# Linear attention on one core: the two PSUM banks of a pair of heads become one tile, and cosine and sine weigh a chunk of both heads in one operation each

## The chip, the cores and the metric

The kernel runs on one core of a Trainium2 chip. The core has five engines that run side by side and meet only at semaphores: TensorE (PE in the profile, with its weight loads as PEld), VectorE (DVE), ScalarE (ACT), GpSimd (POOL) and SyncE (SP, which here only starts transfers). The metric is the device time of one execution in microseconds (us), lower is better.

## The reference

The whole program is four blocks, each an attention-like layer and a feed-forward layer with a layer norm after each. The change lies in the third block's attention, a causal linear attention with 16 heads of 64 features over 4 sequences of 1024 positions:

```python
def cosformer(x, Wq, bq, Wk, bk, Wv, bv, Wo, bo):
    Qp = relu((x @ Wq + bq).reshape(B, T, 16, 64))
    Kp = relu((x @ Wk + bk).reshape(B, T, 16, 64))
    V  = (x @ Wv + bv).reshape(B, T, 16, 64)
    angles = pi / (2 * T) * arange(T)
    cosw, sinw = cos(angles), sin(angles)
    Qc, Qs = Qp * cosw, Qp * sinw
    Kc, Ks = Kp * cosw, Kp * sinw
    # for every position t, over all positions s <= t
    S_cos = cumsum(Kc[s] outer V[s]);  z_cos = cumsum(Kc[s])
    S_sin = cumsum(Ks[s] outer V[s]);  z_sin = cumsum(Ks[s])
    num = Qc @ S_cos + Qs @ S_sin
    den = max(Qc . z_cos + Qs . z_sin, 1e-6)
    return (num / den).reshape(B, T, 1024) @ Wo + bo
```

A position's cosine and sine are the same for all heads and features, so the kernel weighs the values with them before the sum and the result with them after it.

## The kernel before, in words

The stage is `l2_attn`. A *chunk* is 128 positions, a *quarter* two chunks (256 positions), and a *unit* one quarter and one pair of heads (`hp`, 8 pairs). There are 16 quarters, so 128 units. The loop over `t` is a software pipeline written out by hand: in step `t` it issues the projection of unit `t+2`, the key transposes of unit `t+1`, then for unit `t` the matmuls `l2_within` (scores times values inside a chunk) and `l2_before` (query times the state summed over earlier chunks), then scores and state sums of unit `t+1`, then one step of the third block's expert layer where one is ready (`early`), then `l2_out` of unit `t`, and one step of each generator in `side` (the values of the next quarter, the output projection of the last one). TensorE's order is exactly this order (`manual_schedule` for PE alone). The order of the other engines' queues is made by the planner that builds the program, from its own estimate of when each instruction becomes ready.

TensorE leaves the result of a unit in two PSUM banks: `po0` for the first head of the pair, `po1` for the second, each with one buffer. A bank holds, for either chunk, 130 columns: 65 that are to be weighed by the cosine (64 features and the denominator) and 65 by the sine. `l2_out` (L1134 on) takes them out: for each head `i` and each chunk `c`, ScalarE makes `nsin` = sine times its half (L1142, 65 columns a partition), and VectorE makes `num` = cosine times the other half plus `nsin` (L1145). Then VectorE takes the maximum and the reciprocal of the denominators (L1149, L1150) and multiplies (L1151).

The steps that the prediction speaks of, with their lines: `a`, the masked scores, is written by VectorE from the banks `pa0` and `pa1` (L1098), and it comes before `l2_within` of the unit that it belongs to. `state` is written by VectorE from the bank `kp` (L1081, L1083, L1085). The bank `kp` is then filled by the next key transposes (L131), and it is shared with the output of the expert layer; `pa0` and `pa1` are shared with that layer's hidden values (`pa_m` and `kp_mo` in the profile). `cv` is the values: VectorE adds the bias (L1029), ScalarE weighs them by cosine and sine (L1036). ScalarE also makes `r_q` and `r_k` (L1052), `kN` (L1063) and `coT` (L1171). L127 and L131 are helpers that issue matmuls and transposes.

Of the kernel before, what the change touches and what calls it, by code (L numbers as in the profile page):

```python
# [10 lines left out]
F32 = mybir.dt.float32  # L11
I32 = mybir.dt.int32
U32 = mybir.dt.uint32
AF = mybir.ActivationFunctionType
ALU = mybir.AluOpType
# [3 lines left out]
P = 128  # L19
# [14 lines left out]
VW = HD2 + 1  # L34
# [24 lines left out]
class Net:  # L59
# [42 lines left out]
    def load(self, name, shape, pool=None, tag=None, eng=None):  # L102
        pool = pool or self.const
        t = pool.tile(shape, F32, name=f"sb_{name}", tag=tag or f"sb_{name}")
        src = self.io[name]
        (eng or self.nc.sync).dma_start(out=t, in_=src)
        return t
# [811 lines left out]
    def l2_attn(self, load, dispatch, moe):  # L919

        nc, tc = self.nc, self.tc
        NQ = 2
        with ExitStack() as ctx:
            wp = ctx.enter_context(tc.tile_pool(name="cos", bufs=2))
            self.c2["wp"] = wp
            quarters = [  # L930
                dict(b=b, q=q, c0=q * NQ, x=self.xT[b][:, q * NQ * P : (q + 1) * NQ * P])
                for b in range(B)
                for q in range(NC // NQ)
            ]
            units = [dict(Q=Q, hp=hp) for Q in quarters for hp in range(NP2)]
            self.psq = {}
            for t, n in dict(pj=2, po0=1, po1=1, pr=1).items():
                self.psq[t] = ctx.enter_context(
                    tc.tile_pool(name=f"ps_{t}", bufs=n, space=bass.MemoryType.PSUM)
                )  # L940

            two = ctx.enter_context(
                tc.tile_pool(name="ps_two", bufs=1, space=bass.MemoryType.PSUM)
            )
            for t in (("pa0", "m0"), ("pa1", "m1"), ("kp", "mo")):
                v = two.tile([P, 512], F32, name="_".join(t))
                self.psq.update({t[0]: (v, 0), t[1]: (v, 3 * P if t[0] == "kp" else 2 * P)})
            self.mtags = dict(t="pj", h=("m0", "m1"), o="mo")
            self.l2_tiles(quarters[0], None)
            for f in self.l2_values(quarters[0]):  # L950
                pass
            n = len(units)
            side = []

            def early(moe):

                if "done" not in self.m2["st"][1]:
                    for k in range(1):
                        next(moe)


            ctx.enter_context(tc.manual_schedule(engines={mybir.EngineType.PE}))
            for t in range(-2, n + 4):
                if t == 0:
                    load()
                if 0 <= t + 2 < n:
                    u = units[t + 2]
                    self.l2_project(u)
                if 0 <= t + 1 < n:
                    u = units[t + 1]  # L970
                    if u["hp"] == 0:
                        i = (t + 1) // NP2
                        if i + 1 < len(quarters):
                            nxt = quarters[i + 1]
                            self.l2_tiles(nxt, quarters[i])
                            side.append(self.l2_values(nxt))
                    self.l2_keys(u)
                if 0 <= t < n:
                    self.l2_within(units[t])
                    self.l2_before(units[t])  # L980
                if 0 <= t + 1 < n:
                    self.l2_scores(units[t + 1])
                    self.l2_sums(units[t + 1])
                if "put" in self.m2["st"][0] if t > 0 else False:
                    early(moe)
                if 0 <= t < n:
                    self.l2_out(units[t])
                    if t % NP2 == NP2 - 1:
                        Q = units[t]["Q"]
                        side.append(self.l2_project_out(Q))  # L990
                        if Q["c0"] + NQ == NC:
                            side[-1] = chain(side[-1], dispatch(Q["b"]))
                for g in side[:]:
                    if next(g, self) is self:
                        side.remove(g)
            for g in side:
                for f in g:
                    pass
# [104 lines left out]

    def l2_within(self, u):
        Q, hp = u["Q"], u["hp"]
        u["po"] = [self.psb(f"po{i}", [P, 2, 2 * VW], f"po{i}") for i in range(2)]
        for i in range(2):
            for c in range(2):
                self.nc.tensor.matmul(  # L1109
                    out=u["po"][i][:, c, :],  # L1110
                    lhsT=u["a"][:, i, c, :],
                    rhs=Q["v"][c][:, 2 * hp + i, :, :].rearrange("p a d -> p (a d)"),
                    start=c == 0,
                    stop=False,
                    skip_group_check=True,
                )

    def l2_before(self, u):

        Q, hp = u["Q"], u["hp"]  # L1120
        for c in range(1 if Q["q"] == 0 else 0, 2):
            s = slice(c * P, (c + 1) * P)
            for i in range(2):
                h = self.HALF[i]
                self.nc.tensor.matmul(
                    out=u["po"][i][:, c, :],
                    lhsT=u["q"][h, s],
                    rhs=Q["st"][h, hp, c, :],
                    start=False,
                    stop=True,  # L1130
                    skip_group_check=True,
                )

    def l2_out(self, u):  # L1134
        nc, Q, hp, wp = self.nc, u["Q"], u["hp"], self.c2["wp"]
        trig, po = self.c2["trig"], u["po"]
        num = wp.tile([P, 2, 2, VW], F32, name="num")
        for i in range(2):
            for c in range(2):
                k = Q["c0"] + c  # L1140
                t = wp.tile([P, VW], F32, name="nsin", bufs=4)
                nc.scalar.activation(  # L1142
                    t, po[i][:, c, VW : 2 * VW], AF.Copy, scale=trig[:, k, 1:2]
                )
                nc.vector.scalar_tensor_tensor(  # L1145
                    num[:, c, i, :], po[i][:, c, 0:VW], trig[:, k, 0:1], t, ALU.mult, ALU.add
                )
        dn = wp.tile([P, 2, 2, 1], F32, name="dn")
        nc.vector.tensor_scalar_max(dn, num[:, :, :, HD2 : HD2 + 1], 1e-6)  # L1149
        nc.vector.reciprocal(dn, dn)  # L1150
        nc.vector.tensor_mul(  # L1151
            Q["o"][:, :, hp * P : (hp + 1) * P].rearrange("p c (i d) -> p c i d", d=HD2),
            num[:, :, :, 0:HD2],
            dn.to_broadcast([P, 2, 2, HD2]),
        )
# [981 lines left out]
```

## Time and profile before

| what | value |
|---|---|
| time before, median of 4 runs | 2424.82 us (2420.73 to 2429.36) |
| the profiled execution's own time | 2429.53 us |
| its span, first to last instruction | 2427.7 us |
| mean granted TensorE clock in it | 0.910 |
| PE busy over the span | 2084.1 us (86%), PEld 1458.9 us (60%) |
| DVE busy | 1439.8 us (59%) |
| ACT busy | 1334.4 us (55%) |
| POOL busy | 860.5 us (35%) |
| the attention stage, first to last `po` matmul | 646.3 to 1387.2 us |

A row of the profile names a line of the kernel, an engine, an operation and the tiles (output `<-` inputs, buffer numbers left out), then a count, the busy time and the mean duration of one in ns, and the idle time of that engine just before, with what ended it. The numbers that belong to this stage are read from windows of the trace, since shares of the whole span mix stages with different limits. Two `po` rows, `po0` and `po1`, appear as one name.

### The profile page before, as it was taken

Reading aid. Unit: us, or ns where it says so; the run is one execution under the profiler, and the core shown is the slowest. Engines: PE = TensorE matmul, PEld = TensorE weight load, DVE = VectorE, ACT = ScalarE, POOL = GpSimd, SP = SyncE. Lnnn points to the kernel's source line nnn. Section 1 sums busy time; section 2 is a strip of 40 time slices with the busy share of each in tenths; the row PEclk is TensorE's granted clock in tenths of the full one; section 3 lists DMA queues with packets and bytes.
Section 4 is the critical chain, followed back from the end, with each engine's and each line's share of the span. In section 5 each row is a group of like instructions: output and inputs, shape, how many; then the busy total and the mean of one; then the engine's idle time right before and its main releaser. Section 6 shows DMA issues by size and latency. Waiting matters only on the chain. (4 is left out here: it accounts for less than half of the span.)

```text
span 2427.7 us, 35395 instructions
## 1 busy us (share of the span) xinstructions
PE 2084.1 (86%) x12170; PEld 1458.9 (60%) x12170; DVE 1439.8 (59%) x4207; ACT 1334.4 (55%) x2934; POOL 860.5 (35%) x557
## 2 busy tenths in 40 slices
PE   6677879979899999999989965777888989798988
PEld 3455654544577777787768754553455646465666
DVE  7447733433466666755555656676778777676421
ACT  6643433332456566656655555657667776666443
POOL 5001220000000011001021137868888989678400
PEclk9657969979999999999989977987999999898999
DMA  3000110023000010021223156663567766575411
GB/s 101 0 18 22 31 30 9 9 70 86 1 2 1 1 34 21 17 75 42 69 65 88 46 150 189 207 183 91 150 181 186 204 167 183 151 202 153 116 58 48
DMA packets 138516, 209.87 MB, mean 86 GB/s; under 512 B 18597, under 2 KB 75936, under 8 KB 138080
## 3 DMA queue, kind: packets, MB, share of 16 engines
q1 hardware_dynamic: 126048, 172.82, 23.9%
q0 software_dynamic: 12288, 34.79, 6.8%
q8 instruction: 96, 1.57, 0.3%
q14 instruction: 84, 0.69, 0.1%
HBM read 159.24 MB, written 23.16 MB: 75 GB/s over the span
## 5 line engine op out<-in xcount | busy, mean ns | idle before, releaser
L1798 POOL TENSOR_TENSOR hc<-db,cn 128x1024 f32<-128x1024 f32 x128 | 320.4, 2530 | 79.4 <-PE pys L127 30.8
L1782 POOL TENSOR_TENSOR db<-ud,bn 128x1024 f32<-128x1024 f32 x128 | 329.2, 2606 | 44.6 <-DVE pmv L159 16.6
L127 PEld LDWEIGHTS py<-wh,hh 128*128 128x128 f32 x2048 | 249.7, 193 | 80.9 <-issue 41.9
L127 PE MATMUL ph<-xT,wh 128*128 128x512 f32 x512 | 264.4, 637 | 21.0 <-DVE h_acc L1926 6.6
L127 PE MATMUL py<-wh,hh 128*128 128x128 f32 x2048 | 256.5, 278 | 16.3 <-ACT hh L1910 16.0
L1145 DVE SCALAR_TENSOR_TENSOR num<-po,sb_c_trig,nsin 128x65 f32<-128x65 f32 x512 | 132.7, 279 | 231.6 <-ACT nsin L1142 217.7
L1910 ACT ACTIVATE hh<-ph,sb_cols 128x512 f32<-128x512 f32 x256 | 171.2, 681 | 142.8 <-PE ph L127 116.3
L1142 ACT ACTIVATE nsin<-po,sb_c_trig 128x65 f32<-128x65 f32 x512 | 147.9, 315 | 177.3 <-DVE num L1145 103.7
L1786 ACT ACTIVATE da<-dl,aneg 128x512 f32<-128x512 f32 x256 | 175.4, 689 | 72.7 <-DVE db L1787 70.9
L1019 POOL MEMSET cv<- 128x16 f32 x32 | 4.0, 127 | 499.5 <-ACT cv L1036 355.5
L127 PE MATMUL pys<-hc,sb_c_ident 128*128 128x512 f32 x320 | 167.6, 653 | 15.2 <-DMA hc<-hc 15.2
L1926 DVE SCALAR_TENSOR_TENSOR h_acc<-py,gt,h_acc 128x128 f32<-128x128 f32 x256 | 71.9, 343 | 154.4 <-PE py L127 154.4
L127 PEld LDWEIGHTS ph<-xT,wh 128*128 128x128 f32 x512 | 93.3, 202 | 114.2 <-issue 61.0
L1787 DVE TENSOR_TENSOR_SCAN db<-da,carry,db 128x512 f32<-128x512 f32 x128 | 156.8, 1267 | 5.9 <-ACT da L1786 4.3
L1787 DVE TENSOR_TENSOR_SCAN db<-da,db 128x512 f32<-128x512 f32 x128 | 149.8, 1207 | 10.6 <-ACT da L1786 7.9
L127 PE MATMUL pqk<-xT,wE 128*128 128x256 f32 x512 | 136.2, 389 | 7.4 <-DVE cv L1029 6.0
L1359 POOL DMA_INDIRECT xrows<-xN,di x64 | 61.9, 968 | 220.6 <-ACT kN L1063 215.7
L1109 PE MATMUL po<-cv,a 128*128 128x130 f32 x1024 | 136.2, 276 | 0.9 <-DVE num L1145 0.9
L1109 PEld LDWEIGHTS po<-cv,a 128*128 128x128 f32 x1024 | 124.7, 191 | 2.6 <-issue 1.0
L1036 ACT ACTIVATE cv<-cv,sb_c_trig 128x520 f32<-128x520 f32 x128 | 86.4, 724 | 52.1 <-DVE cv L1029 46.7
L127 PEld LDWEIGHTS pys<-hc,sb_c_ident 128*128 128x128 f32 x320 | 63.5, 211 | 84.4 <-issue 62.8
L127 PEld LDWEIGHTS pqk<-xT,wE 128*128 128x128 f32 x512 | 87.6, 190 | 25.1 <-DVE cv L1029 10.1
(430 smaller groups left out, 4445.8 us busy)
## 6 DMA issues: line engine op xcount, KB each, us to landing
wx<-in_wF SPq DMA_DIRECT2D x92, 384.0 KB
wh<-in_wH SPq DMA_DIRECT2D x64, 512.0 KB
bn<-rows SPq DMA_DIRECT2D x128, 256.0 KB
cn<-rows SPq DMA_DIRECT2D x128, 256.0 KB
hc<-hc POOLq DMA_DIRECT2D x48, 512.0 KB
xrows<-zero SPq DMA_DIRECT2D x4, 1472.0 KB
xg<-xrows SPq DMA_DIRECT2D x20, 256.0 KB
yrows<-ys SPq DMA_DIRECT2D x20, 256.0 KB
```

Of the source, the lines that this page charges most:

```text
L127: return self.nc.tensor.matmul(out=out, lhsT=lhsT, rhs=rhs, start=start, stop=stop)
L1036: nc.scalar.activation(Q["v"][c][:, hs, i, :], v1[:, hs, :], AF.Copy, scale=c2["trig"][:, k, i : i + 1],)
L1109: self.nc.tensor.matmul(out=u["po"][i][:, c, :], lhsT=u["a"][:, i, c, :], rhs=Q["v"][c][:, 2 * hp + i, :, :].rearrange("p a d -> p (a d)") ...
L1142: nc.scalar.activation(t, po[i][:, c, VW : 2 * VW], AF.Copy, scale=trig[:, k, 1:2])
L1145: nc.vector.scalar_tensor_tensor(num[:, c, i, :], po[i][:, c, 0:VW], trig[:, k, 0:1], t, ALU.mult, ALU.add)
L1359: i = nc.gpsimd.indirect_dma_start(out=rows[:, :], out_offset=bass.IndirectOffsetOnAxis(ap=st["dest"][k][:, c : c + 1], axis=0), in_=self. ...
L1782: nc.gpsimd.tensor_mul(db, ud, bc[0])
L1786: nc.scalar.activation(da, dl[:, ec, :], AF.Exp, scale=aneg[:, j : j + 1])
L1787: nc.vector.tensor_tensor_scan(db[:, ec, :], da, db[:, ec, :], carry[:, ec, n : n + 1] if h else 0.0, ALU.mult, ALU.add,)
L1798: nc.gpsimd.tensor_mul(hc, db, bc[1])
L1910: nc.scalar.activation(ht, ph, AF.Relu, bias=self.col("h_b1", i=e * NK + k))
L1926: nc.vector.scalar_tensor_tensor(acc[:, c, :], py[:, c, :], gt[:, c, e : e + 1], acc[:, c, :], ALU.mult, ALU.add,)
```

## The change

The two banks of a unit are one tile of two banks, in one pool `po` with one buffer, so PSUM use stays at eight banks. The matmuls that fill it are the same, in the same order. `l2_out` no longer loops over heads: for each chunk, one ScalarE operation weighs the sine half of both heads (2 x 65 columns, from both banks) and one VectorE operation weighs the cosine half of both and adds. A unit has two of each where it had four of each, each of twice the columns. The temporary `nsin` is twice as wide, with two buffers in place of four.

```diff
-            for t, n in dict(pj=2, po0=1, po1=1, pr=1).items():
+            for t, n in dict(pj=2, po=1, pr=1).items():
...
     def l2_within(self, u):
         Q, hp = u["Q"], u["hp"]
-        u["po"] = [self.psb(f"po{i}", [P, 2, 2 * VW], f"po{i}") for i in range(2)]
+
+        po = self.psq["po"].tile([P, 2, 512], F32, name="po")
+        u["po"] = po[:, :, 0 : 4 * VW].rearrange("p i (c d) -> p i c d", c=2)
         for i in range(2):
             for c in range(2):
                 self.nc.tensor.matmul(
-                    out=u["po"][i][:, c, :],
+                    out=u["po"][:, i, c, :],
...
-                    out=u["po"][i][:, c, :],
+                    out=u["po"][:, i, c, :],
                     lhsT=u["q"][h, s],
                     rhs=Q["st"][h, hp, c, :],
...
         num = wp.tile([P, 2, 2, VW], F32, name="num")
-        for i in range(2):
-            for c in range(2):
-                k = Q["c0"] + c
-                t = wp.tile([P, VW], F32, name="nsin", bufs=4)
-                nc.scalar.activation(
-                    t, po[i][:, c, VW : 2 * VW], AF.Copy, scale=trig[:, k, 1:2]
-                )
-                nc.vector.scalar_tensor_tensor(
-                    num[:, c, i, :], po[i][:, c, 0:VW], trig[:, k, 0:1], t, ALU.mult, ALU.add
-                )
+        for c in range(2):
+            k = Q["c0"] + c
+            t = wp.tile([P, 2, VW], F32, name="nsin")
+            nc.scalar.activation(t, po[:, :, c, VW : 2 * VW], AF.Copy, scale=trig[:, k, 1:2])
+            nc.vector.scalar_tensor_tensor(
+                num[:, c], po[:, :, c, 0:VW], trig[:, k, 0:1], t, ALU.mult, ALU.add
+            )
```

## The prediction

> **What bounds the kernel now.** I read the page first, then busy times of the attention stage alone, then what TensorE waited for in it, then the timeline of single units.
>
> ```profile
> L1145 DVE SCALAR_TENSOR_TENSOR num<-po,sb_c_trig,nsin 128x65 f32<-128x65 f32 x512 | 132.7, 279 | 231.6 <-ACT nsin L1142 217.7
> L1926 DVE SCALAR_TENSOR_TENSOR h_acc<-py,gt,h_acc 128x128 f32<-128x128 f32 x256 | 71.9, 343 | 154.4 <-PE py L127 154.4
> L1142 ACT ACTIVATE nsin<-po,sb_c_trig 128x65 f32<-128x65 f32 x512 | 147.9, 315 | 177.3 <-DVE num L1145 103.7
> L1036 ACT ACTIVATE cv<-cv,sb_c_trig 128x520 f32<-128x520 f32 x128 | 86.4, 724 | 52.1 <-DVE cv L1029 46.7
> ```
>
> The page shows the two changed operations as long waits on each other: 217.7 us of VectorE idle before num, 103.7 us of ScalarE idle before nsin. The question is whether TensorE feels it. The busy times from 646 to 1390 us answer that (columns: length, then PE, PEld, DVE, ACT, POOL busy, clock, DMA):
>
> ```profile
> 646.00:1390.00 744.00, 700.01 (x5992) 573.87 (x5990) 461.41 (x1877) 445.20 (x1255) 73.73 (x104) 0.99 0.13 36
> ```
>
> TensorE is busy 700.0 of 744 us; VectorE 62%, ScalarE 60%. Shorter work on those two can return at most TensorE's 44.0 us of idle time, 1.8% of the kernel. TensorE's waits in this window say who ends it:
>
> ```profile
> PE pa_m L127 <- DVE a L1098: 8.1, 11, 1.5
> PE kp_mo L131 <- DVE state L1085: 7.5, 18, 1.9
> PE pqk L127 <- DVE cv L1029: 6.0, 12, 0.6
> PE kp_mo L127 <- ACT kN L1063: 5.9, 8, 2.4
> PE kp_mo L127 <- DVE state L1085: 5.8, 4, 2.3
> ...
> PE po L1109 <- DVE num L1145: 0.9, 1, 0.9
> ```
>
> Only 0.9 us stand against num itself. The others are VectorE and ScalarE work that shares a queue with num and nsin. The timeline of one unit without side work (start, length) shows how:
>
> ```profile
> 713.71 0.32 ACT L1142 ACTIVATE nsin<-po,sb_c_trig 128x65 f32<-128x65 f32 x1 [1.19 <-PE po L1125]
> ...
> 714.06 0.28 DVE L1145 SCALAR_TENSOR_TENSOR num<-po,sb_c_trig,nsin 128x65 f32<-128x65 f32 x1 [1.41 <-ACT nsin L1142]
> 714.26 0.75 DVE L1098 TENSOR_TENSOR a<-pa_m,sb_c_tri 128x256 f32<-128x256 f32 x2
> 714.38 0.52 ACT L1142 ACTIVATE nsin<-po,sb_c_trig 128x65 f32<-128x65 f32 x2 [0.35 <-DVE num L1145]
> ...
> 714.92 0.47 DVE L1145 SCALAR_TENSOR_TENSOR num<-po,sb_c_trig,nsin 128x65 f32<-128x65 f32 x2
> 715.30 0.28 DVE L1083 TENSOR_TENSOR state<-kp_mo,state 128x130 f32<-128x130 f32 x1
> 715.42 0.32 ACT L1142 ACTIVATE nsin<-po,sb_c_trig 128x65 f32<-128x65 f32 x1 [0.52 <-DVE num L1145]
> 715.62 0.29 DVE L1085 TENSOR_TENSOR state<-kp_mo,state 128x130 f32<-128x130 f32 x1
> ```
>
> Here the two engines take turns: the second nsin waits 0.35 us until the first num is done, though both read other columns of the same bank. VectorE's order is num, a, num, num, state, state, num; the last num ends at 716.11, 2.76 us after the unit's last `po` matmul started (713.35). Read the same way for all 128 units, the commonest length of this chain is 2.76 us, and about ten units have 4.1 to 7.8 us. In units with side work the next `po` matmul starts 1.1 us or more after the chain's end; in the others it starts 0.14 us after it or up to 0.37 us before (the first bank is already free).
>
> **The change, part by part.**
>
> *ScalarE.* Out: 512 x 315 ns = 161.3 us. In: 256 operations of 130 columns. Between 65 columns (315) and 520 (724, same kind of scale operand) the slope is 0.90 ns a column, so 315 + 65 x 0.90 = 373 ns; 95.5 us. It saves 66 us of an engine that is 60% busy: nothing by itself, since TensorE covers it; it counts where a TensorE wait ends on ScalarE (kN 5.9, ys 2.0, coT 1.4 us). Bounds of the duration: 315 (columns free) and 2 x 315 = 630 (two banks read one after the other); I take 373, nearest to the L1036 row.
>
> The Trainium skill puts it a little higher: "ScalarE: Activation LUTs", section "What ACT_TABLE_LOAD costs", gives 280 ns + 0.833 ns a column with one pointer operand, 388 ns here. For 65 columns it would be 334, where this trace has 315. By the page a unit saves 560 ns of ScalarE, by the rows 514; both are hidden, so the forecast is the same.
>
> *VectorE.* Out: 512 x 279 = 142.8 us. In: 256 x 345 ns (L1926, the same operation with a column operand and a PSUM input, has 343 at 128 columns) = 88.3 us. 54 us less on an engine that is 62% busy, hidden in the same way. Bounds 279 and 558.
>
> *The chain.* In the unit above, with VectorE's order kept: nsin 713.71 to 714.08, num 714.13 to 714.48, a from 714.40 to 715.15, the second nsin 714.52 to 714.89, the second num 715.07 to 715.42, then the states at 715.33 and 715.65. The chain ends 0.69 us sooner. The last state ends at 715.94, where it ended at 715.91: the first num is 0.07 later by nsin's and num's added columns, the dropped num gives that back. So the transposes into kp that wait for it, the 0.25 us of this unit, stay.
>
> *The buffer.* One tile is free for the next unit only when its last num is done, and the first nsin needs the last matmul of both heads (at most one `po` matmul, 0.13 us between starts, later). In 24 units `po` is now filled before the last num ends, by 6.0 us together (1.35 in one, 0.07 to 0.37 in the rest). With the chain 0.69 shorter only one of them still waits, by 0.66 us at most.
>
> The Trainium skill speaks against this part: "Perfetto Trace Analysis", "Optimizing Tensor Performance", "Matmuls" wants independent matmul groups to rotate through different PSUM banks, so that the evacuation of one overlaps the next group's matmuls, and the change gives up just that. By the rule alone the 6.0 us above would be lost; by the rows the shorter chain more than covers them.
>
> *The sum, on TensorE's waits, VectorE's order kept.*
> - state (7.5 + 5.8 + 1.4 us): the short ones stay; in the few long ones (up to 2.3 us) VectorE had a backlog, and 0.4 us a unit leaves it: 6 x 0.4 = 2.4, taken as -2.5. Bounds 0 and -14.7.
> - cv (6.0 us, 12 waits): in units with values the last num stands right before it and is gone: 0.2 us each, -2.4. Bounds 0 and -6.0.
> - ScalarE's kN, ys, coT (9.3 us, 12 waits): one operation of 0.32 less ahead of the late ones, two longer by 0.06: some 0.15 each, -1.5 rounded down. Bounds 0 and -9.3.
> - num: the 0.9 us wait goes, and in some 20 units without side work `po` starts right behind num instead of 0.06 sooner: -0.9 - 1.2 = -2.1. Bounds +0.7 and -2.1.
> - a (8.1 us on 11 waits; 17.6 us on 32 weight loads): a stands behind the first num, which is 0.07 to 0.2 later: 11 to 32 x 0.12 = +1.3 to +3.8; I take +2. Bounds +6 and, if a comes ahead of num, -8.1.
>
> Sum: -2.5 - 2.4 - 1.5 - 2.1 + 2 = -6.5 us. The bounds add up to +6.7 and -40. From the profiled 2429.53 us (span 2427.7 and 1.8 around it) that is 2423.0; that execution was 4.7 us above the median of the four, so against the median 2424.82 it is 2418.3. Later stages start on this stage's data, so I carry the gain to the end one to one. 0.3% is 7.3 us, about what a measurement of this kernel tells from no change.
>
> **Rivals.**
>
> *The planner moves a and state ahead of num.* The first nsin is longer, so num becomes ready later, while a is ready at 714.1 in the unit above. In that order a runs 714.1 to 714.85, num at 714.77, state by 715.7, 0.25 us sooner. Then the waits on a (8.1) and more than half of those on state (14.7) go: another -8 - 9 us, 2401. For it: VectorE stands idle for 1.41 us before the first num, next to ready work. Against it: in the order of before the num went first, by a margin that I can't see.
>
> *It does nothing.* TensorE is 94% busy, 1.0 of the clock; if the waits on state, a and cv stay, the time is 2424.8 within 3 us. For it: nearly all that is saved lies on idle engines.
>
> *Slower: the first nsin loses its place in ScalarE's queue.* It needs all eight matmuls of two banks, so the planner may see it ready later and put a coT copy (0.57 us) or other work ahead. VectorE's first num then holds a and state up by as much. The unit at 1202.99 shows the price: nsin came 1.39 us after the last matmul started, the chain took 5.67 us and TensorE waited 1.53 us for a. The place is the part with expert work (from about 1020 us on, near 60 units), where pa and kp are shared and a is awaited in 32 units. At 0.57 us in 30 of them it costs 17 us; with the gains on cv, ScalarE and num (-6) the time is 2436. It decides from 0.25 us a unit. Against it: in most units nsin starts 0.36 us after the last `po` matmul with ScalarE idle before.
>
> **How the numbers follow.** Order kept, small gain: 0.42, around 2418 (2412 to 2424), half beyond 0.3%. a and state ahead: 0.18, 2395 to 2412. Nothing: 0.15, 2422 to 2428. Slower: 0.25, 2430 to 2445. Faster is 0.21 + 0.18 = 0.39, same 0.21 + 0.15 = 0.36, slower 0.25. The range leaves a tenth out on each side: 2400 to 2438; the bounds of the sum alone reach from 2385 to 2432.
>
> **What would show it.** nsin and num x256 each, near 373 and 345 ns; VectorE and ScalarE 54 and 66 us less busy in the stage; the commonest chain near 2.07 us; TensorE busy still near 700 us in a stage of some 738. Right at state: the short waits of 0.25 us are still there. Wrong: a wait of TensorE on num above a few us (the buffer), waits on a above 20 us (the slower rival), or waits on a and state both under 5 us (the first rival); or a stage that is as predicted while the time after it has moved, since the planner orders that part too.

## The result, and the profile after

| | median | runs | range |
|---|---|---|---|
| before | 2423.29 us | 70 | 2413.65 to 2434.22 |
| changed | 2420.03 us | 44 | 2411.25 to 2435.75 |

The ratio is 0.9987, with a 95% interval of 0.9977 to 0.9996: the change saves 1 to 6 us of 2423, less than the 0.3% that the prediction takes for what one measurement can tell from no change. The profiled execution took 2419.40 us, with a span of 2417.6 us.

On the page of the changed kernel (columns: line, engine, operation, tiles, shapes, count, then busy us and mean ns of one, then idle time before and what ended it) the two new operations are these:

```profile
L1143 ACT ACTIVATE nsin<-po,sb_c_trig 128x130 f32<-128x130 f32 x256 | 94.6, 369 | 134.5 <-PE po L1127 75.2
...
L1144 DVE SCALAR_TENSOR_TENSOR num<-po,sb_c_trig,nsin 128x130 f32<-128x130 f32 x256 | 89.2, 349 | 275.1 <-ACT nsin L1143 257.2
```

The 130 columns out of two banks cost 369 and 349 ns, where 65 columns cost 315 and 279. The prediction's estimates, without a surcharge for the second bank, were 373 and 345, so none is to be seen. VectorE's busy time in `num` falls from 132.7 to 89.2 us and ScalarE's in `nsin` from 147.9 to 94.6.

The timeline of the changed kernel shows the same chain as the prediction's unit, in another unit without side work (start, length, then engine, line, operation; in brackets the idle time of the engine and what ended it):

```profile
705.65 0.37 ACT L1143 ACTIVATE nsin<-po,sb_c_trig 128x130 f32<-128x130 f32 x1 [1.22 <-PE po L1127]
...
706.05 0.35 DVE L1144 SCALAR_TENSOR_TENSOR num<-po,sb_c_trig,nsin 128x130 f32<-128x130 f32 x1 [2.00 <-ACT nsin L1143]
706.32 0.75 DVE L1098 TENSOR_TENSOR a<-pa_m,sb_c_tri 128x256 f32<-128x256 f32 x2
706.44 0.37 ACT L1143 ACTIVATE nsin<-po,sb_c_trig 128x130 f32<-128x130 f32 x1 [0.42 <-DVE num L1144]
...
706.98 0.35 DVE L1144 SCALAR_TENSOR_TENSOR num<-po,sb_c_trig,nsin 128x130 f32<-128x130 f32 x1
707.24 0.29 DVE L1083 TENSOR_TENSOR state<-kp_mo,state 128x130 f32<-128x130 f32 x1
...
707.56 0.29 DVE L1085 TENSOR_TENSOR state<-kp_mo,state 128x130 f32<-128x130 f32 x1
...
707.91 0.44 PE L131 MATMUL kp_mo<-sb_c_ident,r_k 128*128 128x128 f32 x2 [0.27 <-DVE state L1085]
```

VectorE's order is the one before with two `num` fewer. The chain from the last `po` matmul to the last `num` is now 2.06 us in most units (2.76 before). But TensorE waits for the second `state`, not for `num`, and that wait is still there: 0.27 us where it was 0.25.

What the stage gained is read best from units 0 to 99, ahead of the third block's first gather. These are windows of TensorE, the kernel before and then the changed one (window, its length, then busy us of PE, PEld, DVE, ACT and POOL, the granted clock, the DMA share and GB/s):

```profile
646.26:1202.99 556.73, 532.12 (x4576) 433.30 (x4574) 348.97 (x1397) 335.83 (x937) 41.31 (x68) 1.00 0.09 26
```

```profile
639.60:1190.58 550.98, 531.17 (x4575) 433.48 (x4574) 310.11 (x1197) 298.82 (x737) 41.18 (x68) 1.00 0.09 27
```

VectorE and ScalarE lose 39 and 37 us of busy time; the units get 5.75 us shorter. This gain is not spread over the units. In the common unit `state` comes as late after the last `po` matmul as before (unit 5: 1.98 and 2.29 us, 1.96 and 2.28 before), and the unit is up to 0.02 us longer. Eight units give 5.69 of the 5.75 us: 39 (1.64), 4 (1.07), 71 (0.94), 84 (0.66), 73 (0.58), and 8, 53 and 74 (0.27 each); in the pair of second profiles, b0_before and e8_after below, the same eight give 5.67. In unit 4 the `num` wait of 0.9 us is gone: before, the last `nsin` of unit 3 stood behind `r_q` and `r_k` on ScalarE (665.85 us), and with the shorter chain it stands ahead of them. In unit 39 TensorE's waits were these before, and then with the change:

```profile
PE kp_mo L127 <- ACT kN L1063: 0.8, 1, 0.8
PE pqk L127 <- ACT coT L1171: 0.7, 1, 0.7
PE kp_mo L131 <- DVE state L1085: 0.6, 1, 0.6
```

```profile
PE pqk L127 <- ACT coT L1170: 0.7, 1, 0.7
```

There ScalarE also works for the router: it loads a function table (ACT_TABLE_LOAD, 1.28 us) and makes `rt_l`. Before, both stand behind the unit's `r_k` and hold up `kN`; with the change they are done ahead of `r_q`. e1_swap below, which merges nothing, has them ahead too, and its unit 39 takes 6.09 us (5.87 in the change, 7.51 before); e3_a_first, with the merged operations, has them behind, and its unit takes 7.51 again. So these 1.6 us come from the place of one table load, which the planner chose, and not from the merging as such.

The whole stage gets only 3.2 us shorter (739.5 to 736.3), since units 100 to 106 lose 2.5 (68.5 to 71.1). There the timeline of the changed kernel has, at the first gather:

```profile
1224.74 0.40 ACT L1521 ACTIVATE yg<-yg,wt 128x128 f32<-128x128 f32 x1 [3.44 <-DMA yg<-yrows,di]
1225.05 0.35 ACT L1143 ACTIVATE nsin<-po,sb_c_trig 128x130 f32<-128x130 f32 x1
1225.43 0.35 DVE L1144 SCALAR_TENSOR_TENSOR num<-po,sb_c_trig,nsin 128x130 f32<-128x130 f32 x1 [6.55 <-ACT nsin L1143]
1225.70 0.75 DVE L1098 TENSOR_TENSOR a<-pa_m,sb_c_tri 128x256 f32<-128x256 f32 x2
...
1226.17 2.08 PE L127 MATMUL pa_m<-xgT,wx 128*128 128x128 f32 x8 [2.72 <-DVE a L1098]
```

`yg` is the scaling of rows that a transfer gathers. In the kernel before, the unit's first `nsin` stood ahead of it on ScalarE; now `yg` stands first, waits 3.44 us for the transfer, and `nsin`, `num`, `a` and TensorE wait behind it. The planner turned the two round. The kernel before was held up in the same unit too, one step later: its `yg` stood ahead of the second `nsin`, and TensorE waited for `state` instead of `a`:

```profile
1237.15 0.40 ACT L1522 ACTIVATE yg<-yg,wt 128x128 f32<-128x128 f32 x1 [2.67 <-DMA yg<-yrows,di]
...
1238.86 1.13 PE L127 MATMUL kp_mo<-wx,mh 128*128 128x128 f32 x4 [2.27 <-DVE state L1085]
```

So the new order moves this wait more than it adds to it. In units 100 to 106 TensorE's idle time rises by 0.7 us (12.6 to 13.3); the other 1.8 of the 2.5 us are the same matmuls at a lower granted clock (56.0 us busy at 0.90, 57.8 at 0.88).

TensorE's waits over the whole stage of the changed kernel (us in total, times, longest) are these:

```profile
PE pa_m L127 <- DVE a L1098: 14.9, 33, 2.7
PE kp_mo L131 <- DVE state L1085: 6.9, 17, 1.9
PE pqk L127 <- DVE cv L1029: 6.4, 13, 0.6
PE kp_mo L127 <- ACT kN L1063: 3.9, 5, 2.4
PE kp_mo L127 <- DVE state L1085: 2.6, 2, 1.4
```

Nothing waits for `num` any more. Waits on `a` went from 8.1 us on 11 waits to 14.9 on 33; those on `state` from 14.7 to 10.5. These lists hold waits above 0.15 us. With the shorter ones the waits on `a` are 9.6 us on 32 before and 14.9 on 34 after, so they are nearly all the same waits, each some 0.15 us longer (in units 0 to 99 the same 17), and those on `state` (L1083 and L1085) go from 17.7 on 54 to 10.6 on 21. The two belong together: in a unit such as 77 TensorE waited 0.07 us for `a` and then 0.08 for `state`, and now waits 0.21 for `a` and no longer for `state`.

### The profile page after: what moved, and what is told of

It reads as the page before. It is cut to its first block, busy times and chain, and to the rows that moved or that the text cites. A ratio compares the mean times of both kernels' runs of the same rounds, so it can differ in the third digit from the quotient of the medians.

```text
span 2417.6 us, 34784 instructions
## 1 busy us (share of the span) xinstructions
PE 2076.3 (86%) x12170; PEld 1456.5 (60%) x12170; DVE 1401.8 (58%) x3951; ACT 1287.8 (53%) x2678; POOL 860.3 (36%) x557
## 5 line engine op out<-in xcount | busy, mean ns | idle before, releaser
L1797 POOL TENSOR_TENSOR hc<-db,cn 128x1024 f32<-128x1024 f32 x128 | 326.9, 2582 | 89.7 <-PE pys L127 33.1
L1144 DVE SCALAR_TENSOR_TENSOR num<-po,sb_c_trig,nsin 128x130 f32<-128x130 f32 x256 | 89.2, 349 | 275.1 <-ACT nsin L1143 257.2
L1143 ACT ACTIVATE nsin<-po,sb_c_trig 128x130 f32<-128x130 f32 x256 | 94.6, 369 | 134.5 <-PE po L1127 75.2
L127 PEld LDWEIGHTS ph<-xT,wh 128*128 128x128 f32 x512 | 93.2, 201 | 116.2 <-issue 60.6
L127 PEld LDWEIGHTS pqk<-xT,wE 128*128 128x128 f32 x512 | 87.6, 190 | 25.5 <-DVE cv L1029 10.5
```

The source lines that it names most:

```text
L127: return self.nc.tensor.matmul(out=out, lhsT=lhsT, rhs=rhs, start=start, stop=stop)
L1143: nc.scalar.activation(t, po[:, :, c, VW : 2 * VW], AF.Copy, scale=trig[:, k, 1:2])
L1144: nc.vector.scalar_tensor_tensor(num[:, c], po[:, :, c, 0:VW], trig[:, k, 0:1], t, ALU.mult, ALU.add)
L1797: nc.gpsimd.tensor_mul(hc, db, bc[1])
```

## The experiments

The kernels ran on three chips, each beside runs of the kernel before on the same chip, and each ratio is to those. The kernel before took 2393.46 us beside e0 to e3, 2395.33 beside b0, e5, e7 and e8, and 2424.94 beside e4, e9, e10 and b1. "Stage" is first `po` matmul to the last unit's first one, "behind" the time from there to the end, both from one profile.

| run | ratio to before, 95% | stage | units 100 to 106 | behind |
|---|---|---|---|---|
| before, the first profile | 1 | 739.5 | 68.5 | 1041.9 |
| b0_before | 1.0009 (0.9991 to 1.0027) | 739.7 | 68.8 | 1028.5 |
| b1_before | one run | 740.6 | 68.6 | 1038.6 |
| changed, the first profile | 0.9987 (0.9977 to 0.9996) | 736.3 | 71.1 | 1041.7 |
| e0_again | 0.9958 (0.9939 to 0.9977) | 732.9 | 67.8 | 1018.0 |
| e8_after | 0.9944 (0.9923 to 0.9966) | 733.2 | 68.1 | 1021.3 |
| e1_swap | 0.9983 (0.9967 to 0.9999) | 747.3 | 65.3 | 1013.9 |
| e2_tile_only | 1.0215 (1.0190 to 1.0240) | 793.4 | 64.7 | 1013.2 |
| e3_a_first | 0.9943 (0.9922 to 0.9965) | 725.8 | 63.8 | 1028.4 |
| e5_yg_behind | 0.9887 (0.9865 to 0.9910) | 722.2 | 54.0 | 1023.1 |
| e7_both | 0.9936 (0.9918 to 0.9955) | 717.4 | 52.8 | 1033.5 |
| e9_busy | 0.9987 (0.9971 to 1.0003) | 735.8 | 71.1 | 1036.4 |
| e4_dve_only | 1.0048 (1.0029 to 1.0067) | 743.0 | 70.1 | 1048.9 |
| e10_before_yg | 1.0036 (1.0008 to 1.0065) | 746.4 | 60.6 | 1047.0 |

### The change again, and the kernel before again

No edit: the two kernels as they are, two runs of each.

> The changed kernel as it stands, in a second profile. If the 3.5 us that the unit at the expert layer's first gather (15.90 us long against 12.42 before) lost come from the order of ScalarE's queue (the scaling of the gathered rows stands ahead of the first nsin), that unit is 15 to 16 us again and TensorE's waits on a are again near 15 us. If they were chance of one execution, the unit is 12 to 13 us and those waits are near 10 us. Ratio to before 0.998 to 0.9995 under both.

> The change once more, beside the two runs below. Stage 732 to 737 us, TensorE's waits on a 14 to 15 us, ratio to before 0.995 to 0.9995.

> The kernel before as it stands, for a second profile of it beside the runs below: which of its stages differ from execution to execution. If the attention stage is set by fixed orders, it is again 737 to 741 us long (first to last unit's first po matmul) and only its units around the gathers move by 1 to 3 us, while the stages before and after it follow the granted clock. If the stage moves as the others do, a difference of 3 us in it between two single profiles says nothing.

> The kernel before once more, to see which stretches come back the same. The attention stage: 739.5 to 739.9 us again. The stretch behind it, up to the end, was 1041.9 and 1028.5 us in the two executions of this kernel, 1041.7, 1018.0 and 1021.3 in the three of the changed one. If it belongs to the order of the program and the chip, it is 1027 to 1030 here beside about 1020 for the change; if it is chance of the execution, it is anywhere between 1015 and 1042.

Measured: on the two chips where the kernel before takes 2393 to 2395 us the change is worth 0.4 to 0.6%, where it was 0.13% in the first comparison. Units 0 to 99 agree to 0.02 us: 556.61 to 550.84 here, -5.77, against -5.75 in the first pair of profiles. What differs lies elsewhere. Both ratios are below what was expected (0.998 and 0.995 at the least). Units 100 to 106 give 0.7 here (b0_before and e8_after, one chip) and lost 2.5 there, though `yg` stood ahead of the change's first `nsin` both times: the unit at the first gather takes 15.90 us in the first profile of the change, 14.26 in e0_again and 12.71 in e8_after, and 12.42, 14.68 and 12.57 in the three of the kernel before, while the waits on `a` are 14.4 to 15.0 us each time the change ran. So the order costs waits on `a`, but the loss of 2.5 us is not shown to come from it. Behind the stage the change gained 7.2 us on the chip that ran both, 10.5 across the two faster chips, and nothing in the first pair. Two executions of one kernel there differ by 3.3 us (1018.0 and 1021.3; 1041.9 and 1038.6), and by chip the same kernel before takes 1028.5 or about 1040. The change also reorders that stretch, though it edits nothing in it: by operation and tiles, VectorE's 1334 operations behind the stage stand in one order in b0_before and b1_before, while the longest order that b0_before and e8_after have in common holds 1113. So chance, the chip and the planner's order may all have a part there, and the profiles don't part them.

### One part of the change alone

e2_tile_only has the two banks as one tile and keeps the four operations of 65 columns on each engine:

```diff
-        u["po"] = [self.psb(f"po{i}", [P, 2, 2 * VW], f"po{i}") for i in range(2)]
+        po = self.psq["po"].tile([P, 2, 512], F32, name="po")
+        u["po"] = po[:, :, 0 : 4 * VW].rearrange("p i (c d) -> p i c d", c=2)
```

> One tile of two banks as in the change, but the four nsin and four num of before, in their order. If one tile for two banks has a price of its own (both engines take turns over the whole tile, and TensorE can fill none of it before the last num is done), the chain grows from 2.76 to about 3.4 us, some 50 units have less spare time than that, TensorE waits on num for 15 to 30 us and the kernel is 10 to 30 us slower than before. If banks and tiles do not matter here, it is within 3 us of before.

It is 2.15% slower, and the stage is 54 us longer. The largest row of TensorE's waits in its stage, and two rows of a unit without side work:

```profile
PE po L1111 <- DVE num L1147: 50.1, 55, 2.4
```

```profile
752.14 0.28 DVE L1147 SCALAR_TENSOR_TENSOR num<-po,sb_c_trig,nsin 128x65 f32<-128x65 f32 x1 [0.38 <-ACT nsin L1144]
...
752.57 1.13 PE L1111 MATMUL po<-cv,a 128*128 128x130 f32 x8 [0.42 <-DVE num L1147]
```

With one tile the two engines never read it side by side: in the timeline each `nsin` starts after the last `num` has ended and the other way round, four times over, so the chain is 3.40 us. And the next unit's matmuls wait for the whole tile. The rule that the prediction weighed against the change ("Perfetto Trace Analysis", "Optimizing Tensor Performance", "Matmuls" in the Trainium skill: let independent matmul groups rotate through PSUM banks, so that emptying one overlaps filling the next) agrees with this run: the two banks are still filled in turn, but come free only together, and TensorE waits 50.1 us for them, where it waited 0.9 before. The merged operations, which shorten the chain by 1.34 us, are what makes one tile bearable: with them TensorE waits for `num` nowhere.

e1_swap has the kernel before with its two loops exchanged (chunk outside, head inside), so two tiles and four operations each, in the order of the change:

```diff
-        for i in range(2):
-            for c in range(2):
+        for c in range(2):
+            for i in range(2):
```

> The kernel before with its two loops exchanged: chunk outside, head inside. Still two tiles, four nsin and four num a unit, so no operation is saved; but consecutive operations now go to different banks, so the two engines need not take turns. If the shorter chain is what pays, the commonest chain (last po matmul to the last num's end) falls from 2.76 to about 2.4 us and the time by 1 to 4 us, near that of the change. If the saved operations pay (54 us of VectorE, 66 us of ScalarE), the time stays within 1 us of before.

The chain falls to 2.25 us by this alone, since successive operations read different banks. But VectorE's order becomes num, num, a, a, and the stage is 7.7 us longer than before: waits on `a` are 16.7 us on 33, and on `state` 19.5. A shorter chain at the price of a later `a` and `state` (each some 0.2 us) loses in the stage. (The kernel as a whole is 0.17% faster: the stretch behind the stage was 14.6 us shorter than in b0_before, which ran on the other of the two faster chips. Why is not settled.)

### Is it the freed engine time, or the place in the queue?

e9_busy is meant to give engine time back without touching the chain: behind the second `nsin`, and behind `co`, the unit's last VectorE operation, two operations each that write tiles nobody reads.

```diff
+        for c in range(2):
+            busy = wp.tile([P, 2], F32, name="busyA")
+            nc.scalar.activation(busy, t[:, c, 0:2], AF.Copy, scale=trig[:, k, 1:2])
+            busy = wp.tile([P, 2], F32, name="busyV")
+            with self.tc.issue_after(last):
+                nc.vector.scalar_tensor_tensor(
+                    busy, num[:, c, 0, 0:2], trig[:, k, 0:1], num[:, c, 1, 0:2], ALU.mult, ALU.add
+                )
```

> The change, with two operations more on ScalarE (2 columns, behind the second nsin) and two more on VectorE (2 columns, behind co, the last operation of the pair) for every pair of heads; they write tiles that nobody reads. By the slope of the rows one of 2 columns takes about 316 - 63 x 0.90 = 260 ns on ScalarE and about 215 ns on VectorE, so the stage gets back some 66 us of ScalarE and 55 us of VectorE, about what the change took out, but none of it lies in the chain from the last po matmul to the last num. If the chain and the place of num ahead of state is what the change is worth, the chain stays at 2.06 us and the stage at 733 to 735 us, with the time within 0.2% of the change's (ratio to the kernel before about 0.995). If the worth is in the freed engines (the backlog that my terms for state, cv and ScalarE are built on), the stage goes back to 737 to 740 us, and the waits on state, cv and kN rise again to those of before (14.7, 6.0 and 5.9 us).

They took 294 ns on ScalarE and 215 on VectorE. Units 0 to 99 (columns as above):

```profile
641.96:1192.96 551.00, 531.97 (x4575) 434.69 (x4574) 335.15 (x1397) 345.95 (x937) 41.36 (x68) 1.00 0.09 27
```

ScalarE is busier than in the kernel before (346 against 336 us), and VectorE has 25 of its 39 us back. The units take 551.00 us, as in the change (550.98), and over the whole stage it took 735.8 us, between the two expected ranges, because units 100 to 106 took 71.1, as in the first profile of the change. The ratio is 0.9987, that of the change.

But the equal length is a sum of parts that cancel, so the run does not show that the freed time is worth nothing. The first `nsin` starts 0.32 us after the last `po` matmul, where it starts 0.38 after it in the change; why is not known. The chain is 2.00 us instead of 2.06, and 50 units are some 0.06 us shorter each, 3.0 us together. Against that, units 71, 84, 79 and 40 are 1.8 us longer; 71 and 84 lose 0.78 and 0.52 of the 0.94 and 0.66 that the change had gained there. Unit 53 is 1.5 us longer at a granted clock of 0.71, unit 0 is 0.3 shorter. So of the gain of 5.75 us some 1.3 to 1.8 can be freed engine time, in units where work of other layers queues on ScalarE and VectorE; in the other units giving it back costs nothing. The rest goes with the shorter chain and with orders such as that of the table load in unit 39, which e9_busy keeps.

### Where `a` stands

e3_a_first is the change with both `num` issued behind `a` on VectorE:

```diff
+            with self.tc.issue_after(self.masked):
                 nc.vector.scalar_tensor_tensor(
                     num[:, c], po[:, :, c, 0:VW], trig[:, k, 0:1], t, ALU.mult, ALU.add
                 )
```

> The change, with VectorE's queue ordered so that the masked scores a stand ahead of both num (the planner puts the first num ahead of a). TensorE's waits on a, 14.9 us in the change, should fall below 5 us, the states come 0.1 to 0.2 us sooner, the last num ends 0.2 to 0.3 us later. If those waits are what is left to gain, the time is 5 to 12 us below the change (2408 to 2415 where the change has 2420). If they are only moved on to state, kN or po, it is within 3 us of the change.

TensorE's waits in its stage:

```profile
PE pa_m L127 <- DVE a L1098: 5.2, 5, 1.3
...
PE po L1111 <- DVE num L1145: 3.8, 11, 0.5
PE kp_mo L131 <- DVE state L1085: 2.8, 4, 1.8
```

The waits on `a` fall from 14.9 to 5.2 us. The stage is 7.1 us shorter than in e0_again: 3.3 in units 72 to 99, beside the expert layer, and 4.0 in units 100 to 106. In units 0 to 71 1.4 us are lost: TensorE now waits 1.9 us for `num` there, and unit 39 is 1.6 us longer, with the table load behind `r_k` again. The time, though, equals that of the change (2382.11 and 2382.56 us): the stretch behind the stage was 10 us longer. This is the order of the prediction's first rival, forced: VectorE goes a, a, num, state, state, num, and `state` comes 0.3 us sooner. The 17 us that the rival put on top came as 7 in the stage and as nothing in the time.

Across units 72 to 99 the medians tell what the order does. Counted from the last `po` matmul's start, the first bank of `a` is done after 1.33 us before, 1.46 in the change, 1.35 in e4_dve_only below and 1.17 here, and in these units TensorE waits for `a` for 3.2, 4.7, 3.6 and 1.3 us, short waits included.

### The gather

e5_yg_behind is the change with `yg` ordered behind the unit's last `nsin` on ScalarE, and the output operations of the unit ahead of the expert layer's step in code order:

```diff
+                if 0 <= t < n:
+                    self.l2_out(units[t])
                 if "put" in self.m2["st"][0] if t > 0 else False:
                     early(moe)
...
+                    with self.tc.issue_after(self.nsin):
                         nc.scalar.activation(
```

> The change, with l2_out issued ahead of the expert layer's step (TensorE's order stays as it is) and the scaling of the gathered rows (yg) ordered behind the unit's nsin on ScalarE. If the place of yg ahead of the first nsin is what the change lost, the unit at the first gather falls from 14.3 to 15.9 us to 11 to 12.5, the seven units around it by 3 to 5 us together, and the time by 2 to 4 us against the change. If ScalarE's queue would be waiting there anyway, the seven units stay within 1 us.

Units 104 to 106, of e8_after and then of e5_yg_behind, from the same chip (columns as above):

```profile
1209.17:1247.72 38.55, 30.15 (x202) 24.73 (x201) 20.51 (x93) 22.98 (x59) 15.70 (x18) 0.82 0.25 68
```

```profile
1210.13:1234.59 24.46, 23.76 (x202) 20.10 (x201) 16.17 (x79) 13.47 (x35) 7.80 (x10) 1.00 0.30 85
```

The same 202 matmuls take 38.55 and 24.46 us. 7.7 us of the 14.1 are idle time of TensorE; the other 6.4 are slower matmuls, 30.15 us busy at a granted clock of 0.82 against 23.76 at 1.00. The expectation was 3 to 5 us for the seven units; 14.1 came. This is the fastest kernel of all: 2370.95 us, 1.13% below the kernel before and about 0.5% below the change on that chip. It was measured on that chip alone, and the two parts of the edit, the code order and the place of `yg`, were not tried apart.

e10_before_yg makes the same edit in the kernel before.

> The kernel before (two tiles, four operations each), with the gathered rows' scaling yg ordered behind the unit's last nsin on ScalarE and with the pair's output operations issued ahead of the expert layer's in code order: the edit that took 14 us from units 100 to 106 of the changed kernel (68 to 54 us). If that gain has nothing to do with the change, the same units fall from 68.6 to 54 to 57 us here, the stage from 739.6 to 725 to 729, and the ratio to the kernel before is 0.990 to 0.995. If the gain needs the change's order (yg stands ahead of the first nsin only there), the units stay at 66 to 69 us and the ratio at 1.000 within 0.002.

Both guesses missed: units 100 to 106 fall by 8 us, to 60.6, yet the kernel is 0.36% slower. One unit later in the stage, 112, is 9.4 us longer than in b1_before. ScalarE stands still for 6.0 us there, TensorE for 4.5 and VectorE for 4.2, all up to about 1306 us, with nothing that the profile names as releaser. Units 125 and 126 are another 4.0 us longer, at a granted clock of 0.73 and 0.71. What that is, and whether it comes back in every execution, was not tried. Unit 112 is 2.9 us longer in e5_yg_behind too. So the gain of e5_yg_behind is that of the edit and the change's order together, and not a property of the edit.

e7_both joins the two edits, with `a` ahead of `num` only in units beside the expert layer:

```diff
+            late = "put" in self.m2["st"][0]
+            with self.tc.issue_after(self.masked) if late else nullcontext():
```

> That order of yg, and a ahead of both num, but only in the units that run beside the expert layer (in the others a stays behind the first num, where TensorE waited 3.8 us on num once it was moved). Theory: 33 waits on a of 0.3 us go and none on num comes, so the stage is 717 to 724 us and the time 9 to 14 us below the change. Rival: the place of a costs state and kN what it gives, and the stage is within 4 us of that of the change.

The stage is the shortest of all, 717.4 us, 4.8 below e5_yg_behind as the sum of both edits should have it. The time is about that of the change (2381.18 us, 2383.32 in e8_after): the expected 9 to 14 us did not come. Behind the stage it took 1033.5 us against 1023.1. TensorE's waits there include 19.7 us on `gt` of the last block, but e8_after has 9.5 on `gt` and 10.7 on `yg` at the same transposes, so that row does not tell where the time went. The edits touch no operation of the last block, but its order is another: of some 1330 VectorE operations behind the stage 1110 stand in an order shared with e8_after, and in e3_a_first 1100. Both kernels with `a` ahead of `num` were longer there, by 10 and 12 us, where their stages had gained 7 and 16; whether another order of the last block would keep the gain was not tried.

### Without ScalarE

e4_dve_only leaves ScalarE out: one VectorE multiplication of 520 columns by a broadcast of cosine and sine, and one addition of 260 columns.

```diff
+        nc.vector.tensor_mul(
+            t,
+            po.rearrange("p i c (a d) -> p i (c a) d", a=2),
+            w[:, None, :, None].to_broadcast([P, 2, 4, VW]),
+        )
+        nc.vector.tensor_add(
+            num.rearrange("p c i d -> p i c d"), t[:, :, 0::2, :], t[:, :, 1::2, :]
+        )
```

> The change with VectorE alone: one multiplication of 520 columns out of po by a broadcast of cosine and sine, and one addition of 260 columns; no nsin on ScalarE, so no hand-over between the two engines. By the rows (a: 256 columns in 0.375 us, co: 256 columns in 0.42 us) about 0.7 + 0.4 = 1.1 us a unit where the two num took 0.70. The chain from the last po matmul would be 0.3 + 1.1 = 1.4 us if nothing stands between, 2.2 if a (0.75) does. If the chain counts alone, the stage is 728 to 733 us. If what stands ahead of state and a on VectorE counts, state is later by the whole 1.1 us where it was by 0.70, the waits of TensorE on state rise to 15 to 25 us, and the stage is 736 to 745 us. ScalarE is 95 us less busy either way; if kN, ys and coT are what is late, their 6.5 us of waits fall to 3 or less.

The two operations took 699 and 429 ns. The chain is 1.68 us, the shortest of all. The kernel is 0.48% slower than before, and the stage 743.0 us. Waits on `state` through the key transposes (L131) are 10.4 us, 6.9 in the change. That is not the whole of it: five units (40, 70, 71, 84, 100) ran at a granted clock of 0.79 to 0.90 and are together 6.9 us longer than in the change. One execution of the kernel before in three has such a dip too (unit 53 in b1_before, +1.4 us), so whether this kernel causes its five is open.

## Why the prediction was right, point by point

- *ScalarE and VectorE: right.* 369 and 349 ns came for 373 and 345. The page formula that the prediction set beside it (388 ns, from "ScalarE: Activation LUTs", "What ACT_TABLE_LOAD costs") is 5% above the measured 369. The engine time saved is smaller than predicted, 53 us for 66 and 44 for 54: count times mean counts overlapping pairs twice (two `num` in a row took 0.47 us, not 0.56). That this time is hidden was right in the main: given back in e9_busy, it costs 1.8 us in four units.
- *The chain: right.* 2.06 us for 2.07, and the 0.25 us wait behind `state` stayed as 0.27.
- *The buffer: right.* TensorE waits for the tile nowhere. e2_tile_only shows what the cover was worth: with the old operations, 50.1 us.
- *The sum: near, by parts that were not, so with luck.* All waits of the stage counted, the short ones too, its terms came so: ScalarE's -1.5 as -2.6 us (9.2 to 6.6), `a` +2 as +5.2 (9.6 to 14.9), `num` -2.1 as -0.9, `state` -2.5 as -7.1 (17.7 to 10.6), `cv` -2.4 as +0.4 (6.0 to 6.4), and waits that it did not name +1.0. TensorE's idle time falls by 4.0 us (43.5 to 39.5), its busy time rises by 0.8. In units 0 to 99 alone the terms are -1.4, +0.9, -0.9, -3.3 and -0.2, idle time falls by 4.8 us and busy time by 0.9.
- *The step that was mis-sized* is the pair `a` and `state`. The step of 0.12 us on `a` was right (0.14 measured), but it was counted nearer to the 11 waits of the list than to the 32 of the weight loads, and the trace has 32. It stays within its bound of +6. For `state` "the short ones stay" holds for those of 0.25 us; of the shorter ones, 3.1 us on 30 waits, one of 0.15 us is left. Beside the expert layer the longer wait on `a` ahead of them takes them in. And the term for `cv` failed: its waits fall by 0.12 us in units such as 7 and 15 but rise by as much in 23, 55 and 87, and units 100 to 106 add 0.6.
- *The slower rival's kind* did come, at one place: at the gather a first `nsin` loses its place on ScalarE, behind `yg` and not behind `coT`. In units 100 to 106 the waits on `a` rose from 3.3 to 6.4 us, those on `state` fell from 5.4 to 2.6. Its price of 17 us did not come.
- *The backlog* by which the terms for `state` and `cv` were argued ("0.4 us a unit leaves it") is real, but in few units: five units with a queue that is backed up (39, 71, 73, 74, 84) give 4.1 us, of which 1.6 go with the order of the table load.
- *The other rivals.* The planner did not put `a` and `state` ahead of `num`; forced in e3_a_first, that order shortens the stage by 7 us and not the kernel. "It does nothing" is refuted for units 0 to 99 (-5.75 and -5.77), and close for the total of the first comparison.
- *The size: half.* -6.5 us was predicted, and the medians differ by -3.3: units 0 to 99 gave -5.75 and units 100 to 106 took 2.5 back, 1.8 of it at a lower clock.
- *From the stage to the end, one to one:* not so. The stretch behind the stage moved by -10 to 0 us with the change. Its order, the chip and chance may each set that, and how much each gives of the 0.4 to 0.6% on the faster chips stays open.

## What to carry to other kernels

Two banks as one tile, read by two engines in turn, cost 51 us here by themselves and pay only with operations that are merged by as much; price both halves of such an edit apart. Read an operation that frees an engine for what stands behind it in that engine's queue, not for its busy time: 37 to 39 us of two engines gave at most some 1.8 us, in units where a queue was backed up, while one table load in another place gave 1.6. Compare unit by unit before a total is explained: the gain lay in eight of 100 units, and the equal lengths of two kernels hid 3 us each way. And look for an operation that waits on a transfer and was moved ahead of ready work: with `yg` ordered behind `nsin`, units 104 to 106 of the changed kernel were 14 us shorter, more than the whole change.

## What the runs showed of the hardware

- The granted clock can be low in a stretch with waits, and the matmuls then take longer: the same 202 matmuls took 23.76 us busy at a clock of 1.00, with 0.7 us of idle time, and 30.15 at 0.82, with 8.4. That is no rule: unit 105 ran at 1.00 with 2.96 us of idle time in e0_again and at 0.86 with 2.62 in e8_after, and unit 116 of both at 1.00 with 2.7. What sets it is open.
- The granted clock also dips without a wait: unit 40 of e4_dve_only, where TensorE was busy in all of its 8.10 us, ran at 0.79, against 6.60 us at 1.00 in the change, and unit 53 of b1_before at 0.73 in 6.02 us, against 4.61 in the other two profiles of that kernel.
- The chips differ: the kernel before took 2393 to 2395 us on two and 2423 to 2425 in the other comparisons; 19 us of it lie ahead of the attention stage (627.2 against 646.3) and 10 to 13 behind it, and none in it (739.7 against 739.5).
